# Hats from one product: offsets in three parts, positions and distance on 62 rows of a column of taps

## The chip, the core and the metric

The kernel runs on one core of a Trainium2 chip. The metric is the device time of one launch in microseconds (us), the median of three runs. One more execution was taken with the hardware profiler; its span is 7707.8 us, and all views of the profile are of that execution.

## The reference

Two layers work on x of 2 x 256 x 128 x 128 in fp32. What the change touches is in the first: a group norm, then three branches of deformable depthwise convolution with the dilations 1, 9 and 12. Each branch computes 18 offset planes by a 3x3 convolution (a y and an x offset for each of 9 taps), samples the normalised image bilinearly at the shifted positions, weighs the taps and sums them.

```python
def _branch(x, w_off, w_def, lw, lb, pad, dil):
    off = _conv(x, w_off, pad, dil)
    y = _deform_dw(x, off, w_def, pad, dil)   # bilinear samples at py, px, weighted per tap
    return jax.nn.gelu(_ln2d(y, lw, lb), approximate=False)
py = yy - pad + ky * dil + off[:, :, 0]
px = xx - pad + kx * dil + off[:, :, 1]
```

The branches and a 1x1 convolution are added, normalised, sent through an MLP and added to x. The second layer is a group norm and a 3x3 convolution with ternary weights.

## The kernel before

The kernel has three stages, one after the other. In the first (phase_a, for image 0 and then image 1) every group of four rows is normalised (tile xa), transposed by TensorE (tpa) and stored in a table of pixels (function columns); the same xa is multiplied with the weights of the offset convolutions (pz, copied to the ring zr). Every eight rows offsets adds up rows of zr (zs), shifts them by products with shift (po), and has 54 offsets for each pixel of eight rows (offs: 128 pixels of a row on the partitions, 8 rows, 54 planes).

A bilinear weight is a hat, 1 - min(1, |d|), of the distance d between a sampling position and a grid place. make_hats computes the weights of four rows (512 pixels) at all candidate places of all taps. The distance is linear: offset, plus where the pixel lies in a pattern of period 2 in y or 10 in x, plus a constant that depends on the place. So it is a product of a 0/1 matrix (hatw) with a matrix that has these numbers on its rows (planes). So that bf16 loses nothing, an offset is split in three bf16 parts which are added up by the product. The split is made on VectorE (DVE) at L395 to L398: round, subtract, round the rest, subtract. Parts are laid out with pixels on the partitions, so TensorE transposes them (pp, L407 and L408), and DVE copies the result to planes (L410, L411). pp, planes and hatw have two layers: in layer 0 the first parts of the 54 offsets and, from row 64, the second parts; in layer 1 the third parts and, from row 64, eight pattern rows. A layer of hatw has 648 columns: 27 taps with 24 places each.

For each of 3 columns of taps and 2 subsets of the 9 rows of taps (4 or 5) there is one bank of ph, made by two products that add up:

```python
for i, m in ((0, P), (1, HALF + NPAT)):
    nc.tensor.matmul(
        ph[0:n],
        lhsT=k["hatw"][0:m, i, h0 : h0 + n],
        rhs=pl[0:m, i, :],
        start=i == 0,
        stop=i == 1,
    )
```

The first takes 128 rows, the second 72. ScalarE (ACT) takes the absolute value (hb, L427), DVE does min and subtract (L428), and SyncE (SP) stores the bank to the array hats (L429). ph has two banks, pp one, hb eight buffers.

The order of the first stage is set by the framework's scheduler, which places each engine's instructions in a queue when the program is built; each engine runs its queue in order and waits by semaphores. At the end of the stage a flag is computed from the largest offset of both images, and the program branches on it. The second stage (sample_near) loads hats and table and does the sampling and what follows; its order on PE, ACT and DVE is written out by hand. The third is the second layer's convolution.

Of the kernel before, what the change touches and what calls it, by code (L numbers as in the profile page):

```python
# [19 lines left out]
P = 128  # L20
# [47 lines left out]
def conv_preact_kernel(ctx: ExitStack, tc: tile.TileContext, t: dict, out: bass.AP):  # L68
# [208 lines left out]
    def phase_a(b, pool, psum, k, beside):  # L277
# [53 lines left out]
        def offsets(G):  # L331


            po = psum.tile([P, 512], F32, name="po", tag="po", bufs=1)
            pov = po[:, 0 : ZG * NOFF].rearrange("p (r n) -> p r n", n=NOFF)
            zs = pool.tile([P, 3, ZG, 3 * 18], F32, name="zs", tag="zs", bufs=2)
            for br, dil in enumerate(DILS):

                def rows(ky, y, y1):

                    y, y1 = max(y, -ky * dil), min(y1, H - ky * dil)
                    while y < y1:
                        s = (y + ky * dil) % ZRING
                        n = min(y1 - y, ZRING - s)
                        z0 = (br * 3 + ky + 1) * 54
                        yield y, n, zr[:, s : s + n, z0 : z0 + 54]
                        y += n

                y0, y1 = G * ZG, (G + 1) * ZG
                for y, n, mid in rows(0, y0, y1):  # L350
                    done = y
                    for ya, na, up in rows(-1, y, y + n):
                        if ya > done:
                            nc.vector.tensor_copy(
                                zs[:, br, done - y0 : ya - y0], mid[:, done - y : ya - y]
                            )
                        nc.vector.tensor_tensor(
                            zs[:, br, ya - y0 : ya - y0 + na], mid[:, ya - y : ya - y + na], up,
                            ALU.add,
                        )  # L360
                        done = ya + na
                    if done < y + n:
                        nc.vector.tensor_copy(
                            zs[:, br, done - y0 : y + n - y0], mid[:, done - y : n]
                        )
                for y, n, down in rows(1, y0, y1):
                    dst = zs[:, br, y - y0 : y - y0 + n]
                    nc.vector.tensor_tensor(dst, dst, down, ALU.add)
            for br, dil in enumerate(DILS):
                for kx in range(3):  # L370
                    nc.tensor.matmul(
                        pov[:, :, br * 18 : br * 18 + 18],
                        lhsT=k["shift"][:, k["dxs"].index((kx - 1) * dil), :],
                        rhs=zs[:, br, :, kx * 18 : kx * 18 + 18],
                        start=br == 0 and kx == 0,
                        stop=br == 2 and kx == 2,
                    )
            offs = pool.tile([P, ZG, NOFF], F32, name="offs", tag="offs", bufs=2)
            nc.vector.tensor_copy(offs.rearrange("p r n -> p (r n)"), po[:, 0 : ZG * NOFF])
            i = b * (H // ZG) + G  # L380
            nc.vector.tensor_reduce(
                amax[:, i : i + 1],
                offs.rearrange("p r n -> p (r n)"),
                AX.X,
                ALU.max,
                apply_absolute_value=True,
            )
            nc.sync.dma_start(
                offd[b][G * ZG : (G + 1) * ZG].rearrange("r w n -> w r n"), offs
            )  # L390

            parts = k["parts"][G % 2]
            rest = pool.tile([P, ZG, NOFF], F32, name="rest", tag="rest", bufs=2)
            first, second = parts[:, 0, :, 0:NOFF], parts[:, 0, :, HALF : HALF + NOFF]
            nc.vector.tensor_copy(first, offs)  # L395
            nc.vector.tensor_tensor(rest, offs, first, ALU.subtract)
            nc.vector.tensor_copy(second, rest)
            nc.vector.tensor_tensor(parts[:, 1, :, 0:NOFF], rest, second, ALU.subtract)  # L398
            return parts

        def make_hats(g, parts, r0):


            pp = psum.tile([P, 2, NG], BF16, name="pp", tag="pp", bufs=1)
            for r in range(R):
                cols = slice(r * W, (r + 1) * W)
                nc.tensor.transpose(pp[:, 0, cols], parts[:, 0, r0 + r, :], ident_b)  # L407
                nc.tensor.transpose(pp[0:HALF, 1, cols], parts[:, 1, r0 + r, 0:HALF], ident_b)  # L408
            pl = k["planes"][g % 2]
            nc.vector.tensor_copy(pl[:, 0, :], pp[:, 0, :])  # L410
            nc.vector.tensor_copy(pl[0:HALF, 1, :], pp[0:HALF, 1, :])  # L411
            for tap in range(3):
                q0 = 0
                for nq in (4, 5):
                    n = nq * NH
                    h0 = (tap * 9 + q0) * NH
                    ph = psum.tile([P, 512], F32, name="ph", tag="ph", bufs=2)
                    for i, m in ((0, P), (1, HALF + NPAT)):
                        nc.tensor.matmul(  # L419
                            ph[0:n],  # L420
                            lhsT=k["hatw"][0:m, i, h0 : h0 + n],
                            rhs=pl[0:m, i, :],
                            start=i == 0,
                            stop=i == 1,
                        )
                    hb = pool.tile([P, NG], F32, name="hb", tag="hb", bufs=8)
                    nc.scalar.activation(hb[0:n], ph[0:n], AF.Abs)  # L427
                    nc.vector.tensor_scalar(hb[0:n], hb[0:n], 1.0, 1.0, ALU.min, ALU.subtract)  # L428
                    nc.sync.dma_start(  # L429
                        hats[b][q0 : q0 + nq, :, g * R : (g + 1) * R, tap].rearrange(  # L430
                            "q h r w -> (q h) r w"
                        ),
                        hb[0:n].rearrange("h (r w) -> h r w", w=W),
                    )
                    q0 += nq
# [11 lines left out]
    with ExitStack() as actx:  # L447
        psum = actx.enter_context(tc.tile_pool(name="ps_a", bufs=1, space=PSUM))

        def gps():  # L450
# [6 lines left out]
            "zero": ap.tile([P, C], F32, name="zero"),  # L457
            "wz": ap.tile([P, KC, NZ], F32, name="wz"),
            "shift": ap.tile([P, len(dxs), P], F32, name="shift"),
            "hatw": ap.tile([P, 2, NTAP * NH], BF16, name="hatw"),  # L460
            "parts": [ap.tile([P, 2, ZG, P], BF16, name=f"parts{i}") for i in range(2)],
            "zr": ap.tile([P, ZRING, NZ], F32, name="zr"),
            "planes": [ap.tile([P, 2, NG], BF16, name=f"planes{i}") for i in range(2)],
        }
# [5 lines left out]
        for b in range(NB):  # L470
            stats = ap.tile([P, KC, NGRP, 6], F32, name=f"stats1_{b}", tag=f"stats1_{b}")
            for c in range(KC):
                for g0 in range(0, NGRP, XT):
                    xt = ap.tile([P, XT * NG], F32, name="xt", tag="xt", bufs=3)
                    nc.sync.dma_start(
                        xt,
                        x[b, c * P : (c + 1) * P].rearrange("p h w -> p (h w)")[
                            :, g0 * NG : (g0 + XT) * NG
                        ],
                    )  # L480
                    for j in range(XT):
                        nc.vector.bn_stats(stats[:, c, g0 + j, :], xt[:, j * NG : (j + 1) * NG])
            if b == 0:
                load_now()
                nc.sync.dma_start(k["wz"], t["wz"].rearrange("(k p) n -> p k n", p=P))
                nc.sync.dma_start(k["shift"], t["shift"])
                hatw = ap.tile([P, 2, NTAP * NH], F32, name="hatw32", tag="xt", bufs=3)
                nc.sync.dma_start(hatw, t["hatw"])
                nc.vector.tensor_copy(k["hatw"], hatw)
                pattern = ap.tile([P, NG], F32, name="pattern", tag="xt", bufs=3)  # L490
                nc.sync.dma_start(pattern[HALF : HALF + NPAT], t["pattern"])
                for pl in k["planes"]:
                    nc.vector.tensor_copy(
                        pl[HALF : HALF + NPAT, 1, :], pattern[HALF : HALF + NPAT]
                    )
            mean, rstd = group_norm(stats, f"gn1_{b}", gps)
            gn1.append((mean, rstd))

            nc.vector.tensor_scalar(negmean[b], mean, -1.0, None, ALU.mult)
            for c in range(KC):  # L500
                nc.vector.tensor_scalar(
                    convs[b][:, c, :], convs[b][:, c, :], rstd[:, c : c + 1], None, ALU.mult
                )
            phase_a(b, ap, psum, k, beside)
# [810 lines left out]
```

## Time and profile before

| what | value |
|---|---|
| median of three runs | 7720.23 us (7712.4 to 7721.3) |
| span of the profiled execution | 7707.8 us |
| ph products L419 | 768, first at 115.3 us, last at 943.5 us |
| hats on ACT, L427 | 384, median 593 ns |
| transposes L407 and L408 | 256 each |
| casts L395 and L397, subtractions L396 and L398 | 32 each, medians 375, 377, 602 and 598 ns |
| PE, DVE, ACT busy over the whole span | 92%, 80%, 63% |

A line of a timeline gives the start in us, the duration in us, the engine, the line of the kernel, the operation, the tiles and how many instructions were merged. PE is TensorE's multiplication and PEld its loading of weights. The form 128*96 says that 128 rows and 96 columns of the array are active. A product's duration on PE contains its latency, so products in a row overlap in the record. In windows, "busy (x)" is the time in us in which an engine was busy and the number of its instructions. A product of fp32 stands as two records. The shares of busy time over the whole span mix three stages, so windows of the first stage are what counts here.

### The profile page before, as it was taken

Reading aid. Unit: us, or ns where it says so; the run is one execution under the profiler, and the core shown is the slowest. Engines: PE = TensorE matmul, PEld = TensorE weight load, DVE = VectorE, ACT = ScalarE, POOL = GpSimd, SP = SyncE. Lnnn points to the kernel's source line nnn. Section 1 sums busy time; section 2 is a strip of 40 time slices with the busy share of each in tenths; the row PEclk is TensorE's granted clock in tenths of the full one; section 3 lists DMA queues with packets and bytes.
Section 4 is the critical chain, followed back from the end, with each engine's and each line's share of the span. In section 5 each row is a group of like instructions: output and inputs, shape, how many; then the busy total and the mean of one; then the engine's idle time right before and its main releaser. Section 6 shows DMA issues by size and latency. Waiting matters only on the chain. (4 is left out here: it accounts for less than half of the span.)

```text
span 7707.8 us, 115349 instructions
## 1 busy us (share of the span) xinstructions
PE 7056.2 (92%) x37984; PEld 5364.4 (70%) x37984; DVE 6136.7 (80%) x12907; ACT 4821.4 (63%) x10150; POOL 716.3 (9%) x1292
## 2 busy tenths in 40 slices
PE   6899888999999999999988999999999999899999
PEld 3455477877877787877777877877788877444444
DVE  7666658888888888888578888888888886677676
ACT  2344356777777777777666777777777777433232
POOL 0000000111111111111100111111111111000000
PEclk9899989999999999999999999999999999899999
DMA  9867699999999999998689999999999996222121
GB/s 296 242 188 200 181 233 252 243 254 257 248 250 254 255 246 249 248 255 228 190 232 249 250 250 258 248 251 252 251 249 251 246 250 172 86 77 73 71 74 49
DMA packets 1012350, 1658.94 MB, mean 215 GB/s; under 512 B 120672, under 2 KB 573072, under 8 KB 1007512
## 3 DMA queue, kind: packets, MB, share of 16 engines
q1 hardware_dynamic: 994328, 1617.86, 78.2%
q10 hardware_dynamic: 17408, 33.56, 1.3%
q8 instruction: 304, 4.98, 0.3%
q14 instruction: 310, 2.54, 0.1%
HBM read 1381.02 MB, written 270.06 MB: 214 GB/s over the span
## 5 line engine op out<-in xcount | busy, mean ns | idle before, releaser
L886 PE MATMUL pm<-A,xs 128*128 128x180 f32 (+2 forms) x22288 | 3603.7, 317 | 467.9 <-ACT ev L895 435.2
L886 PEld LDWEIGHTS pm<-A,xs 128*128 128x128 f32 x22288 | 3399.3, 195 | 684.4 <-ACT ev L895 543.7
L864 DVE SCALAR_TENSOR_TENSOR ring<-ev,defw,ring 128x256 f32<-128x256 f32 (+3 forms) x6272 | 2775.7, 462 | 358.6 <-ACT ev L895 173.4
L895 ACT COPY ev<-pm 128x360 f32<-128x360 f32 (+2 forms) x5572 | 2238.5, 455 | 1125.7 <-DVE ring L864 453.7
L813 DVE TENSOR_TENSOR A<-hy,hx 128x768 f32<-128x768 f32 x1130 | 1021.3, 946 | 417.4 <-DMA hx<-hats 238.6
L1169 PE MATMUL pc<-cring,signs 128*128 128x512 bf16 x4608 | 1007.5, 382 | 20.0 <-ACT cring L1116 13.3
L1169 PEld LDWEIGHTS <-signs 128*128 128x128 bf16 x4608 | 452.4, 98 | 574.5 <-issue 30.1
L611 ACT ACTIVATE T<-T,rs 128x256 f32<-128x256 f32 x1280 | 662.4, 593 | 3.3 <-POOL rs L607 3.2
L604 POOL TENSOR_SCALAR rs<-mv 128x4 f32<-128x4 f32 x320 | 122.5, 383 | 4962.3 <-DVE mv L602 2297.5
L570 PE MATMUL hp<-T,w 128*128 128x512 f32 x1024 | 493.1, 606 | 13.8 <-ACT T L689 13.8
L600 DVE BATCH_NORM_STATS2 st<-T 128x6 f32<-128x256 f32 x1280 | 447.0, 412 | 24.0 <-ACT T L592 23.9
L320 PE MATMUL pz<-wz,xa 128*128 128x486 f32 x1024 | 462.8, 585 | 1.3 <-DVE zr L327 1.3
L570 PE MATMUL h<-hT,w 128*128 128x512 f32 x1024 | 460.1, 592 | 0.0
L639 ACT ACTIVATE T<-zc,bb,bw 128x512 f32<-128x512 f32 x384 | 279.2, 782 | 219.8 <-PE zc L623 215.4
L857 ACT ACTIVATE ring<-ev,defw 128x256 f32<-128x256 f32 (+1 forms) x788 | 392.2, 503 | 24.1
L623 PEld LDWEIGHTS zc<-ident,T 128*128 128x128 f32 x2560 | 323.4, 150 | 97.2 <-issue 61.4
L1177 ACT ACTIVATE o<-xl,l1b 128x1024 f32<-128x1024 f32 x64 | 73.5, 1148 | 502.0 <-DMA out_x<-o 384.6
L623 PE MATMUL zc<-ident,T 128*128 128x128 f32 x2560 | 365.9, 287 | 20.2 <-ACT T L611 14.1
L606 POOL TENSOR_TENSOR rs<-rs,mhalf 128x4 f32<-128x4 f32 x320 | 371.3, 1160 | 0.0
L1116 ACT CAST cring<-D 128x2048 bf16<-128x2048 f32 (+1 forms) x140 | 245.0, 1755 | 185.0 <-PE pc L1169 127.6
L592 ACT COPY T<-tp 128x512 f32<-128x512 f32 x640 | 341.9, 590 | 29.5 <-PE tp L590 29.2
L427 ACT ACTIVATE hb<-ph 96x512 f32<-96x512 f32 (+1 forms) x384 | 211.2, 592 | 183.0 <-PE ph L419 177.0
(118 smaller groups left out, 5258.8 us busy)
## 6 DMA issues: line engine op xcount, KB each, us to landing
hy<-hats SPq DMA_DIRECT2D x1114, 384.0 KB
hx<-hats SPq DMA_DIRECT2D x1114, 384.0 KB
xs<-table SPq DMA_DIRECT2D x1876, 128.0 KB
g12d<-T SPq DMA_DIRECT2D x128, 512.0 KB
other<-g12d SPq DMA_DIRECT2D x128, 512.0 KB
hats<-hb SPq DMA_DIRECT2D x192, 240.0 KB
hats<-hb SPq DMA_DIRECT2D x192, 192.0 KB
xl<-x1d SPq DMA_DIRECT2D x56, 640.0 KB
```

The costliest lines, as they stand in the source:

```text
L320: nc.tensor.matmul(pz[:, 0:NZ], lhsT=xt[:, c, r, :], rhs=k["wz"][:, c, :], start=c == 0, stop=c == KC - 1,)
L570: nc.tensor.matmul(out, lhsT=w, rhs=v, start=i == 0, stop=i == n - 1)
L600: pin(nc.vector.bn_stats(st[:, j, :], Tv[:, j, :]))
L606: nc.gpsimd.tensor_tensor(rs[:, 0, :], rs[:, 0, :], mhalf[:, 0:NB4], ALU.pow)
L611: nc.scalar.activation(Tv[:, j, :], Tv[:, j, :], AF.Identity, scale=rs[:, 0, j : j + 1], bias=rs[:, 1, j : j + 1],)
L623: nc.tensor.transpose(zc[:, j * P : (j + 1) * P], Tv[:, j, c * P : (c + 1) * P], ident)
L813: nc.vector.tensor_tensor(dst, hy[:, i0:i1].rearrange("p i t w -> p t i w"), hx[:, i0:i1].rearrange("p i t w -> p t i w"), ALU.mult,)
L857: pin(nc.scalar.mul(dst, src, w))
L864: pin(nc.vector.scalar_tensor_tensor(dst, src, w, dst, ALU.mult, ALU.add))
L886: nc.tensor.matmul(pm[:, j, 0:n], lhsT=xts[b, Rt][T + j][:, c * P : (c + 1) * P], rhs=A[:, m0:m1, AO + (T + j) * CI : AO + (T + j + 1) * C ...
L895: nc.scalar.copy(ev[:, m0:m1, T * CI : (T + 2) * CI].rearrange("p m (t j) -> p t m j", j=CI), pm[:, :, 0:n].rearrange("p t (m j) -> p t m ...
L1169: nc.tensor.matmul(pc[:, bank, :], lhsT=w[:, m * P : (m + 1) * P], rhs=xc[:, i, k, t * JC : (t + 1) * JC, kx : kx + W], start=j == 0, stop ...
```

## The change

The 54 offsets are ordered by column of taps: (n x) -> x n with x = 3. A column of taps has 18 offset planes. A block of 64 rows now holds all that this column's hats are made of: 18 first parts, 18 second parts, 18 third parts and 8 pattern rows, 62 rows in all. Blocks 0 and 1 lie on rows 0 to 63 and 64 to 127 of layer 0 of planes, block 2 on rows 0 to 63 of layer 1. A bank of ph is made by one product with 64 rows, at row 0 for columns 0 and 2 and at row 64 for column 1. The pattern no longer lies in planes but in parts, with pixels on the partitions, and is transposed with the offsets. hatw has one layer.

```diff
-            first, second = parts[:, 0, :, 0:NOFF], parts[:, 0, :, HALF : HALF + NOFF]
-            nc.vector.tensor_copy(first, offs)
-            nc.vector.tensor_tensor(rest, offs, first, ALU.subtract)
-            nc.vector.tensor_copy(second, rest)
-            nc.vector.tensor_tensor(parts[:, 1, :, 0:NOFF], rest, second, ALU.subtract)
+            blocks = parts.rearrange("p r (x n) -> p r x n", n=HALF)
+
+            def taken(i):
+                return blocks[:, :, :, i * (NOFF // 3) : (i + 1) * (NOFF // 3)]
+
+            def by_column(v):
+                return v.rearrange("p r (n x) -> p r x n", x=3)
+
+            nc.vector.tensor_copy(taken(0), by_column(offs))
+            nc.vector.tensor_tensor(by_column(rest), by_column(offs), taken(0), ALU.subtract)
+            nc.vector.tensor_copy(taken(1), by_column(rest))
+            nc.vector.tensor_tensor(taken(2), by_column(rest), taken(1), ALU.subtract)
...
-                nc.tensor.transpose(pp[:, 0, cols], parts[:, 0, r0 + r, :], ident_b)
-                nc.tensor.transpose(pp[0:HALF, 1, cols], parts[:, 1, r0 + r, 0:HALF], ident_b)
+                nc.tensor.transpose(pp[:, 0, cols], parts[:, r0 + r, 0 : 2 * HALF], ident_b)
+                nc.tensor.transpose(
+                    pp[0:HALF, 1, cols], parts[:, r0 + r, 2 * HALF : 3 * HALF], ident_b
+                )
...
-                    for i, m in ((0, P), (1, HALF + NPAT)):
-                        nc.tensor.matmul(
-                            ph[0:n],
-                            lhsT=k["hatw"][0:m, i, h0 : h0 + n],
-                            rhs=pl[0:m, i, :],
-                            start=i == 0,
-                            stop=i == 1,
-                        )
+                    rows = slice(tap % 2 * HALF, (tap % 2 + 1) * HALF)
+                    nc.tensor.matmul(
+                        ph[0:n],
+                        lhsT=k["hatw"][rows, h0 : h0 + n],
+                        rhs=pl[rows, tap // 2, :],
+                        start=True,
+                        stop=True,
+                    )
...
-            "hatw": ap.tile([P, 2, NTAP * NH], BF16, name="hatw"),
-            "parts": [ap.tile([P, 2, ZG, P], BF16, name=f"parts{i}") for i in range(2)],
+            "hatw": ap.tile([P, NTAP * NH], BF16, name="hatw"),
+            "parts": [ap.tile([P, ZG, 3 * HALF], BF16, name=f"parts{i}") for i in range(2)],
...
-                pattern = ap.tile([P, NG], F32, name="pattern", tag="xt", bufs=3)
-                nc.sync.dma_start(pattern[HALF : HALF + NPAT], t["pattern"])
-                for pl in k["planes"]:
-                    nc.vector.tensor_copy(
-                        pl[HALF : HALF + NPAT, 1, :], pattern[HALF : HALF + NPAT]
-                    )
+                pattern = ap.tile([P, ZG, NPAT], F32, name="pattern", tag="xt", bufs=3)
+                nc.sync.dma_start(pattern, t["pattern"])
+                for parts in k["parts"]:
+                    for i in range(3):
+                        at = i * HALF + NOFF
+                        nc.vector.tensor_copy(parts[:, :, at : at + NPAT], pattern)
```

The rest of the diff fills pattern and hatw on the host in the new order.

More of the change, by code (lines that the diff above doesn't have):

```diff
@@ L486, in conv_preact_kernel @@
                 nc.sync.dma_start(k["shift"], t["shift"])
-                hatw = ap.tile([P, 2, NTAP * NH], F32, name="hatw32", tag="xt", bufs=3)
+                hatw = ap.tile([P, NTAP * NH], F32, name="hatw32", tag="xt", bufs=3)
                 nc.sync.dma_start(hatw, t["hatw"])
                 nc.vector.tensor_copy(k["hatw"], hatw)
-                pattern = ap.tile([P, NG], F32, name="pattern", tag="xt", bufs=3)
-                nc.sync.dma_start(pattern[HALF : HALF + NPAT], t["pattern"])
-                for pl in k["planes"]:
-                    nc.vector.tensor_copy(
-                        pl[HALF : HALF + NPAT, 1, :], pattern[HALF : HALF + NPAT]
-                    )
+                pattern = ap.tile([P, ZG, NPAT], F32, name="pattern", tag="xt", bufs=3)
[4 more added lines that the diff above has]
+                        nc.vector.tensor_copy(parts[:, :, at : at + NPAT], pattern)
             mean, rstd = group_norm(stats, f"gn1_{b}", gps)
@@ L1250 @@
     shift = np.stack([px[:, None] == px[None, :] + dx for dx in dxs], 1).astype(np.float32)
-    pattern = np.ones((NPAT, R, W), np.float32)
+    pattern = np.ones((W, ZG, NPAT), np.float32)
     for m in range(RI):
-        pattern[m] = ((np.arange(R) + REACH + m) % RI)[:, None]
+        pattern[:, :, m] = ((np.arange(ZG) + REACH + m) % RI)[None, :]
     for i, m in enumerate(XCLS):
-        pattern[RI + i] = ((np.arange(W) + REACH + m) % CI)[None, :]
-    hatw = np.zeros((P, 2, NTAP * NH), np.float32)
+        pattern[:, :, RI + i] = ((np.arange(W) + REACH + m) % CI)[:, None]
+    hatw = np.zeros((P, NTAP * NH), np.float32)
     ybase = np.zeros((H, NTAP), np.float32)
@@ L1263 @@
             for comp, size, m in ((0, TR, dy % RI), (1, TC, RI + XCLS.index(dx % CI))):
-                plane = br * 18 + comp * 9 + tap
+                base = tap % 3 % 2 * HALF
+                plane = (br * 18 + comp * 9 + tap) // 3
                 for r in range(size):
                     h = (n % 3 * 9 + n // 3) * NH + comp * TR + r
-                    hatw[[plane, HALF + plane], 0, h] = 1.0
-                    hatw[[plane, HALF + m], 1, h] = 1.0
-                    hatw[HALF + NPAT - 1, 1, h] = REACH - r
+                    for part in range(3):
+                        hatw[base + part * (NOFF // 3) + plane, h] = 1.0
+                    hatw[base + NOFF + m, h] = 1.0
+                    hatw[base + NOFF + NPAT - 1, h] = REACH - r
             ybase[:, n] = np.arange(H) + dy
@@ L1277 @@
         "shift": shift,
-        "pattern": pattern.reshape(-1, NG),
+        "pattern": pattern,
         "hatw": hatw,
```

## The prediction

> **What bounds the kernel now.** I first looked for the stage that holds the change. The tile view of ph gives its instructions between 115 and 944 us of the 7707.8 us span, and none later; this is the first stage, in which both images are normalised, transposed and turned into hats. Then I asked for the busy time in windows of that stage.
>
> ```profile
> core 0: us, PE busy (x) PEld busy (x) DVE busy (x) ACT busy (x) POOL busy (x), PEclk, DMA share, GB/s
> ...
> 600.00:700.00 100.00, 99.66 (x416) 56.50 (x416) 66.00 (x149) 42.37 (x79) 0.00 (x0) 1.00 0.72 196
> 700.00:800.00 100.00, 99.69 (x419) 56.46 (x418) 64.29 (x144) 42.52 (x80) 0.00 (x0) 1.00 0.71 196
> ...
> 900.00:950.00 50.00, 39.69 (x189) 22.31 (x188) 31.81 (x77) 22.19 (x40) 0.78 (x1) 0.95 0.72 183
> 240.00:400.00 160.00, 138.72 (x531) 74.63 (x530) 111.72 (x237) 53.70 (x102) 0.00 (x0) 0.91 0.81 238
> ```
>
> In the second image PE is busy 99.7 of 100 us at full clock, with DVE at 65, ACT at 42 and DMA at 0.72. A round of eight rows (two calls of columns, one of offsets, two of make_hats) takes 25.6 us from one L395 to the next, and 20 of the 32 rounds have about that period. Elsewhere PE is not the limit: between 240 and 400 us it is busy 139 of 160, DVE waits there for xa's loads, and rounds take 33 us; after 920 us ACT and the stores of hats set the pace. The next stage reads a flag made from all offsets and the hats of both images, so what the PE-bound rounds lose or win moves the end one for one. Later stages have the same instructions on PE, DVE, ACT and SP in both programs, in the same order.
>
> Then the price of a hat product, from the tile view of ph:
>
> ```profile
> L419 PE MATMUL ph<-planes,hatw x768: 376/379/634, 115.3 to 943.5; 128*96 128x512 bf16 x192
> L427 ACT ACTIVATE hb<-ph x384: 583/593/622, 116.2 to 944.0; 96x512 f32<-96x512 f32 x192
> ```
>
> A product is recorded with 379 ns, but that holds its latency. What it costs PE is the step from start to start: four in a row last 1.03 us, so (1.03 - 0.38) / 3 = 0.217 us. Four products also keep their loads (PEld) out of the way.
>
> Last, what it costs PE to change the shape of the tile that it computes on. The change makes ph run on 64 rows; no product here does that yet. But L408 does on columns: it writes 64 of 128. The PE timeline of one piece shows it:
>
> ```profile
> 494.95 0.64 PE L419 MATMUL ph<-planes,hatw 128*96 128x512 bf16 x2
> 495.42 0.22 PE L407 MATMUL pp<-ident_b,parts 128*128 128x128 bf16 x1
> 495.48 0.59 PE L419 MATMUL ph<-planes,hatw 128*120 128x512 bf16 x2
> 496.00 0.24 PE L408 MATMUL pp<-ident_b,parts 128*64 128x128 bf16 x1
> 496.18 0.23 PE L407 MATMUL pp<-ident_b,parts 128*128 128x128 bf16 x1
> ...
> 492.33 0.24 PE L408 MATMUL pp<-ident_b,parts 128*64 128x128 bf16 x1
> 492.50 1.08 PE L320 MATMUL pz<-wz,xa 128*128 128x486 f32 x2
> ```
>
> L407, 128 columns wide like its neighbours, hands over after 0.06 us (495.42 to 495.48). The second ph of 495.48 starts at 495.48 + 0.59 - 0.38 = 495.69, and L408 follows at 496.00: 0.31 us instead of 0.217, so 0.09 us to enter the other shape. L408 itself takes 0.17 us (492.33 to 492.50) where a stream of 128 columns took 0.06: 0.11 us, of which I put some 0.02 to its own load and 0.09 to leaving. And the first pass of pz after it lasts 1.08 - 0.57 = 0.51 us, against 0.98 - 0.57 = 0.41 in undisturbed pairs: 0.10 us, because its load could not run ahead. A ph after L408 loses 0.04 us that way.
>
> [...] loads of hatw start some 0.4 us ahead behind a pz. [...] the casts with a step of 3 should stay at 0.375 us.
>
> **The change part by part.**
>
> Removed: one of two products per bank of ph, 384 x 0.217 = -83.3 us of PE. ACT still makes 384 hats at 0.593 us and the stores are the same.
>
> Added: visits to a 64-row tile. In the order of the changed program the 384 products stand in 239 groups (115 single, 120 of two, a few longer) between whole-array instructions. A visit costs 0.09 to enter, 0.04 for its own load, 0.09 to leave, and the exposed load of what follows. 179 visits end at pz, tpa or po (fp32, 0.10): 0.32 us each, 58 us. 35 end at a transpose of L407's kind, behind which the next load starts after 0.06 us and which I give 0.02: 0.24 each, 8 us. 25 end, but for one, at a transpose of L408's kind, which had to be entered from another shape anyway: 0.14, 4 us. Together +70 us, from neighbours on the other axis: the bounds are 0 (rows need no drain) and 153 us (below).
>
> Gained beside it: at 51 places a product on rows 64 to 127 meets one on rows 0 to 63 in the same shape. If they run side by side each hides one: -11 us, or 0 if not. I take -11.
>
> PE's balance is -83 + 70 - 11 = -24 us. Only the PE-bound rounds give it to the end; with 20 of 32 fully and a few in part I take 0.7: -17 us.
>
> Moved: transposes. Each first transpose now needs the third part too, so DVE's chain from po to pp grows by the last subtraction (L398 before), 0.60 us: 0.61 + 0.60 + 0.38 + 0.60 + 0.38 + 0.60 = 3.2 us, and 0.66 for a zr copy between. The changed order puts 8 tpa and 5 pz (4.9 us) there instead of 8 and 3 (3.3 us), so the 0.2 us that L407 waits in a full round (at 622.20 us pz hands over to it after 0.60 us instead of 0.41) should go: -4 us in 20 rounds. Queued behind a late transpose are pz and ph, and ACT behind those; so in the last two rounds of each image, where nothing stands between, it costs 4 x 0.6 = +2 us.
>
> On DVE, the casts could [...] take the 0.60 us of the subtraction: up to 2 x 0.22 us per round, in an engine that is 65% busy and with 0.8 us of room: 0 to +3 us, I take 0. The six copies of pattern and the cast of half as many weights lie between 67 and 100 us, hidden by pz: 0 (bounds -1 to +1). hatw's load is 324 KB smaller; nothing waits for it (cast at 67.2, first use at 115), but DMA is 0.9 busy there: 0 to -2 us, I take -1. The smaller memset of parts is hidden by the first loads. No queue is passed by another on SP but the stores of hats and table, which change places with each other.
>
> Sum: -17 - 4 + 2 - 1 = -20 us. On this execution's span 7707.8 becomes 7688; the three timed runs (7712.4 to 7721.3) have a median 12.4 us above that span, so 7720 becomes 7700.
>
> **The rivals.** *Rows are free.* A 64-row tile could need no drain. For it: only columns are shown to drain. [...] Then PE would lose 94 us; in bursts of hats ACT then binds (two hats and half a zr copy, 1.19 + 0.28 us, against 0.43 + 0.81 of PE), so about 0.6 of it reaches the end: -55 us, 7665.
>
> *Rows drain dearer, and the kernel is slower.* The place is each of the 239 visits: if the array empties fully, entering and leaving cost the whole latency beyond the stream[...] and both loads (0.12 and 0.19) lie bare: 0.64 us, 153 us in all, against 83 saved with no overlap: +70, of which 0.7 reaches the end, 7769. The balance turns at 94 / 239 = 0.39 us a visit, or 0.35 without overlap; I have 0.29 on average. With 0.45 it would be 7738. For it: the margin is thin. Against it: L408 shows less.
>
> *The saving is hidden.* If xa's loads and DVE set more of the rounds than I think, or ACT's banks of ph (two) become the wait, nothing moves: 7715 to 7722. Against it are the windows with PE at 99.7.
>
> **How the numbers follow.** Drain as with columns: 0.55, spread 7685 to 7715. Rows free: 0.20. Dearer drain: 0.18. Hidden: 0.07. A measurement of this kernel tells 0.2% (15 us) from no change. Faster by more: 0.31 of the first case, all of the second, 0.01 of the last: 0.52. Within: 0.23 + 0.05 = 0.28. Slower: 0.01 + 0.18 + 0.01 = 0.20. The likeliest case's own range is 7685 to 7715; for 8 in 10 the range takes in most of the free case and the nearer half of the dear one, 7650 to 7745.
>
> **What would show it.** Right: in the PE timeline, pz to ph in 0.50 us, ph's last to pz in about 0.31 to 0.35, pz's first pass 0.51; a full round of 25.0 us or a little less instead of 25.6; rows 64 followed by rows 0 within some 10 ns. The drain is wrong if loads of hatw still start ahead behind pz, or if those steps exceed 0.6 us. The whole argument is wrong if the time after 950 us changes, or if PE is no longer over 95% busy in the second image while the rounds still last 25.6 us.

## The result, and the profile after

The changed kernel takes 7757.0 us (median of four runs, 7753.8 to 7758.4), beside 7720.8 for the kernel before (7712.4 to 7721.4). The ratio is 1.0049, interval 1.0031 to 1.0066: slower by half a per cent. The forecast was faster, 7700 us, and the measured time lies above its range, which ended at 7745. The profiled execution of the changed kernel has a span of 7755.9 us, 48.2 more than before's.

All of that arises in the first stage. The last hat on ACT ends at 993.6 us where it ended at 944.6, 49 us later; from there to the end it takes 6762.2 us, and took 6763.2. The first 13 rounds of each image took 379 and 333 us before and take 388 and 360; the stretch from the first image's last split to the second image's first grew from 57 to 68. Over all rounds, some 25 of the 49 us lie in the second image, 8 in the first, 11 in that stretch and 4 after the last split.

The windows of the first stage, as for the kernel before (columns: window and length; PE, PEld, DVE, ACT, POOL busy; PE clock; DMA share; GB/s):

```profile
600.00:700.00 100.00, 95.22 (x348) 46.44 (x348) 63.92 (x141) 40.24 (x76) 0.00 (x0) 0.95 0.72 197
700.00:800.00 100.00, 96.99 (x349) 45.80 (x350) 63.41 (x140) 41.31 (x77) 0.00 (x0) 0.95 0.67 182
800.00:900.00 100.00, 92.52 (x323) 44.27 (x321) 56.87 (x123) 34.05 (x63) 0.00 (x0) 0.88 0.62 168
```

PE is no longer busy throughout (99.7 before), and its clock, which was 1.00, is 0.88 to 0.95. At half clock two passes of pz take 1.99 us where they otherwise take 1.08 (both below), and PE counts as busy throughout, so the first number hides part of the loss. DVE and ACT are busy for less of each window than before, and DMA for no more: no other engine has become full over a window. Something interrupts PE. Its waits between 560 and 900 us name what (line waited for: us in total, times, longest):

```profile
DVE xa L173 <- DMA xa<-in_x: 17.7, 16, 2.9
PE pz L320 <- DVE zr L327: 15.0, 11, 3.1
```

PE waits 11 times until DVE has copied a bank of pz to zr. Before, that wait did not occur there at all, and DVE's wait for xa's loads was 13.1 us in 12 times. Two timelines show the chain. First the kernel before; "SPq" and "ACTq" lines are DMA issues, a "x12" is twelve of them from the start given:

```profile
602.81 11.06 SPq L429 DMA_DIRECT2D hats<-hb  x12
...
608.69 0.39 ACTq L296 DMA_DIRECT2D xa<-in_x  x1
...
613.51 0.55 DVE L173 TENSOR_SCALAR xa<-xa,gn_mean,gn_rstd 128x512 f32<-128x512 f32 x1 [0.56 <-DMA xa<-in_x]
...
617.18 0.37 ACTq L296 DMA_DIRECT2D xa<-in_x  x1
...
620.65 0.38 DVE L395 CAST parts<-offs 128x432 bf16<-128x432 f32 x1
620.94 0.54 DVE L173 TENSOR_SCALAR xa<-xa,gn_mean,gn_rstd 128x512 f32<-128x512 f32 x1
```

A round loads xa twice. DVE waits for the first of the two, here 0.56 us at 613.51; all 12 waits of the kernel before between 560 and 900 us are for a first load, and PE does not feel them. The second load goes out at 617.18, 8.5 us after the first and some 4 us after the last store of hats. DVE needs it inside the split, at 620.94, and finds it there. Between 617.2 and 621 the DMA share is 0.53. Now the changed kernel:

```profile
812.32 10.23 SPq L438 DMA_DIRECT2D hats<-hb  x11
...
819.42 0.37 ACTq L296 DMA_DIRECT2D xa<-in_x  x1
...
824.36 1.38 SPq L438 DMA_DIRECT2D hats<-hb  x1
...
825.79 0.38 ACTq L296 DMA_DIRECT2D xa<-in_x  x1
...
829.26 0.44 DVE L402 CAST parts<-offs 128x432 bf16<-128x432 f32 x1
...
832.10 0.55 DVE L173 TENSOR_SCALAR xa<-xa,gn_mean,gn_rstd 128x512 f32<-128x512 f32 x1 [2.40 <-DMA xa<-in_x]
...
834.01 0.67 DVE L327 COPY zr<-pz 128x486 f32<-128x486 f32 x1
834.73 1.29 PE L320 MATMUL pz<-wz,xa 128*128 128x486 f32 x2 [2.53 <-DVE zr L327]
...
837.70 1.99 PE L320 MATMUL pz<-wz,xa 128*128 128x486 f32 x2
```

The second load goes out 6.4 us after the first and 1.4 us after the last hats store was issued; the DMA share until 832.1 is 0.87. DVE waits 2.40 us for it at its place in the split, the zr copy queued behind comes late, and PE, which needs that bank, stands 2.53 us. In each of the nine rounds from 604 to 832 us DVE waits so for the second load. From soon after PE's wait to 856 us PE runs at half clock: the two passes of pz at 837.70 take 1.99 us, where undisturbed ones take 1.08.

### The profile page after: what moved, and what is told of

The parts are those of the page before. It is cut to its first block, busy times and chain, and to the rows that moved or that the text cites. A ratio compares the mean times of both kernels' runs of the same rounds, so it can differ in the third digit from the quotient of the medians.

```text
span 7755.9 us, 114589 instructions
## 1 busy us (share of the span) xinstructions
PE 7084.5 (91%) x37600; PEld 5313.8 (69%) x37600; DVE 6148.2 (79%) x12911; ACT 4818.5 (62%) x10150; POOL 713.4 (9%) x1292
## 5 line engine op out<-in xcount | busy, mean ns | idle before, releaser
L320 PE MATMUL pz<-wz,xa 128*128 128x486 f32 x1024 | 513.1, 629 | 46.2 <-DVE zr L327 46.1
```

The lines of the kernel that those rows point to most:

```text
L320: nc.tensor.matmul(pz[:, 0:NZ], lhsT=xt[:, c, r, :], rhs=k["wz"][:, c, :], start=c == 0, stop=c == KC - 1,)
```

## The experiments

Three explanations were open: that visits to a 64-row tile are dearer than priced; that DVE holds PE up (its slower split, or the order with five pz between po and the transposes); that xa's loads come late. Ratios are to the kernel before in the same series of runs. Single runs of one kernel spread widely (the kernel before from 7693 to 7745 us in a series of 63), so only the intervals tell how firm a difference is.

**One product on all 128 rows.** hatw holds zeros in the rows of the other column, rows 64 to 127 of layer 1 of planes are cleared once, and a bank is still one product, with no visit to another shape.

```diff
-                        lhsT=k["hatw"][rows, h0 : h0 + n],
-                        rhs=pl[rows, tap // 2, :],
+                        lhsT=k["hatw"][:, h0 : h0 + n],
+                        rhs=pl[:, tap // 2, :],
...
+        for pl in k["planes"]:
+            nc.vector.memset(pl[HALF:, 1, :], 0.0)
```

> The changed kernel, with the one product of each bank of ph on all 128 rows (the other column's rows of hatw are zero, rows 64 to 127 of the second layer of planes are zeroed once). The same numbers are computed and the order on PE is that of the changed kernel, but no product changes the shape of the tile. Theory A (the visits to 64 rows ate what the removed products saved; the rest of the loss is DVE's wait for xa, which lets PE stall on zr and its clock halve): the steps pz to ph 0.41 instead of 0.50 us, ph to pz 0.22 instead of 0.35; PE has 60 us less to do (71 of visits less, 11 of side-by-side products given back), but the waits for zr and the spells at half clock stay, so 7757 becomes about 7715, with at least three spells of half clock left in the second image. Theory B (64 rows by themselves make the clock drop): no spell of half clock in the second image, about 7680. Theory C (DVE's slower strided split is the loss): waits as before the edit, about 7715 too, told apart by the third run.

Measured: 7689.5 us, 0.9963 (0.9953 to 0.9972), some 67 us below the changed kernel. That is near what the prediction gave the visits (70 less 11), but the waits differ in the two kernels, so it is no clean price; the rounds below give one. But this kernel has 2.6 us less PE work in each round than before by the same working, 83 us in all, and gains only 29. Its waits between 560 and 900 us:

```profile
DVE xa L173 <- DMA xa<-in_x: 35.7, 16, 4.1
PE pz L320 <- DVE zr L327: 32.5, 11, 4.2
```

Both waits are twice as long as in the changed kernel, with no 64-row tile anywhere. The less PE has to do, the longer they are. The clock is 0.90 to 0.93 in the windows from 560 to 860 us, so 64-row tiles are not what lowers it; the time itself lies between what I expected with the spells of half clock (7715) and without them (7680).

**A fifth buffer for xa**, in the changed kernel and, as a control, in the kernel before.

```diff
-            xt = pool.tile([P, KC, R, W], F32, name="xa", tag="xa", bufs=4)
+            xt = pool.tile([P, KC, R, W], F32, name="xa", tag="xa", bufs=5)
```

> The changed kernel with five buffers for xa instead of four, so that each load is asked for one group of rows earlier; PE's order is the same. Theory A: DVE's waits for xa and PE's waits for zr over 1 us vanish in the second image, the clock stays at 1.0 there, rounds of 25.0 us or less; 7757 becomes 7705 to 7730. Theory B: the waits vanish but the clock still drops, 7745 to 7757. Theory C: 7745 to 7757 with waits of PE for zr left.

> Control: the kernel before with five buffers for xa. Its second image has hardly a wait to lose (25.6 us a round), so only the rounds of 33 us in the first image shorten: up to 5 x 7 us, 7690 to 7715. If it gains as much as the changed kernel does by the same edit, the late loads are no property of the change.

Measured: 7749.3 us, 1.0043 (1.0032 to 1.0054), and for the control 7717.5 us, 1.0001 (0.9991 to 1.0012). In the changed kernel PE still waits 12.7 us for zr copies, and a load is still normalised 5 to 6 us after its issue: the scheduler moved the normalisation with the load. The experiment did not take the wait away, and decides nothing on it. The changed kernel's time fell where I had put the other theories, the control's 2 us above what I expected.

**The split read contiguously.** The planes stand in the wrong order by this, so the hats are computed from other taps' offsets; work and shapes are the same.

```diff
-                return v.rearrange("p r (n x) -> p r x n", x=3)
+                return v.rearrange("p r (x n) -> p r x n", x=3)
```

> The changed kernel with the split reading offs and rest in their own order (18 neighbours at a time instead of every third). The planes then come in the wrong order, so the hats are of other taps' offsets; the work is the same. Theory C: the casts return to 0.375 and the subtractions to 0.60 us, 0.42 us less per round in front of zr and pp; PE's waits for zr and the spells of half clock vanish and the time falls by 20 us or more. Theories A and B: the durations fall, the time by at most 13 us (32 rounds of 0.42), 7744 to 7757.

Measured: 7736.7 us, 1.0032 (1.0021 to 1.0043). Casts and subtractions are back at 377, 379, 602 and 601 ns. That is 13 us less than the changed kernel by the ratios, though their intervals overlap; PE still waits 11.8 us in 10 times for zr copies. The step of 3 costs something, and is not the main cause.

**Loads in a tile of their own.** Three buffers take the loads and two the normalised groups, so a load is issued about a round ahead, and the scheduler puts both normalisations ahead of the split. The same in the kernel before.

```diff
-            xt = pool.tile([P, KC, R, W], F32, name="xa", tag="xa", bufs=4)
+            xl = pool.tile([P, KC, R, W], F32, name="xl", tag="xl", bufs=3)
+            xt = pool.tile([P, KC, R, W], F32, name="xa", tag="xa", bufs=2)
...
-                normalise(xt[:, c], xt[:, c], mean[:, c : c + 1], rstd[:, c : c + 1])
+                normalise(xt[:, c], xl[:, c], mean[:, c : c + 1], rstd[:, c : c + 1])
```

> The changed kernel with xa in two tiles: loads go to xl (three buffers), the normalised rows to xa (two buffers). DVE's order then has no normalisation between the split's four steps, and a load has some 12 us before it is needed. The edit before it (a fifth buffer) had left the load and the wait where they were, 5 to 6 us apart. Theory A (late loads hold DVE, DVE holds PE on zr, and after a stall of over some 1.4 us PE runs at half clock for 10 to 20 us): PE's waits for zr over 1 us and the spells of half clock are gone from the rounds of the second image, which take 24.4 to 25.0 us; 7700 +- 10, 40 to 60 us less than the changed kernel. Theory B (64 rows make the clock drop): spells stay, 7735 or more. Theory C (the split's own slower steps): stalls and spells stay in half the rounds, 7730.

> Control: the kernel before with the same two tiles. Its second image stays at 25.6 us a round; in the first image the five rounds of 33 us shorten where the late loads caused them, by 0 to 30 us: 7690 to 7716. The prediction's balance of PE work (24 us for the change) is tested by the difference of the run beside it and this one: 10 to 24 us in favour of the change if the sum was right and only the waits were missed; against the change by 10 us or more if the visits cost more than was counted.

Measured: the changed kernel with it 7678.1 us, 0.9955 (0.9938 to 0.9973); the kernel before with it 7673.0 us, 0.9962 (0.9948 to 0.9976). Late loads had cost the kernel before 0.38% (29 us, most of it in the first image, whose rounds fell from 33 to 25 to 29 us) and the changed kernel 0.94% (73 us). The difference, 44 us, is more than the 38 us by which the change lost; the intervals leave some 20 us of doubt on it. Both kernels are faster than I expected, and the 10 to 24 us in favour of the change that I expected between them did not show: it is 5 us by the ratios, and 5 us against the change by the medians. In the changed kernel's second image the clock is back at 1.00, no wait for zr is left, and PE's largest wait is that for the split, about once a round:

```profile
PE pp L415 <- DVE parts L406: 4.7, 14, 1.3
```

This edit takes the normalisations out of the split too. Their place alone is not the cause: in the kernel before they stand in the split as well (620.94 above), and PE does not wait.

**All zr copies on ACT**, in the changed kernel with its loads as they were, so that the wait cannot go by way of DVE's zr copies.

```diff
-                (nc.scalar.copy if r % 2 else nc.vector.tensor_copy)(
+                nc.scalar.copy(
```

> The changed kernel with all copies of pz to zr on ACT (half of them were on DVE). DVE still waits for the loads of xa in the middle of the split, but it no longer frees pz's banks. If PE is held only by way of zr, its waits of over 1 us and the spells of half clock go: 7690 to 7715. If DVE's wait reaches PE by the split as well (pp waits for the last subtraction), waits of 1 to 2 us for parts appear in their place and spells of half clock stay: 7725 to 7755.

Measured: 7739.4 us, 1.0026 (1.0016 to 1.0037). No wait for a zr copy on DVE is left, and the wait comes by another way:

```profile
DVE xa L173 <- DMA xa<-in_x: 53.8, 15, 5.5
...
PE po L371 <- DVE zs L368: 12.0, 11, 1.7
```

DVE waits longer for xa than in any other kernel, and PE waits for the sums zs queued behind. It is the first load of a round that is late here: one goes out at 598.08, 0.06 us after a hats store, and is normalised at 604.18, after a wait of 4.38 us. The second load follows the last hats store by some 4 us and is on time in all rounds but one. Moving the copies gave back 18 us of the loss by the ratios (the intervals overlap), and the profiled execution has a clock of 1.00 from 560 to 860 us. Late loads reach PE by more than one way.

**The order alone.** In the kernel before, the transpose of the third parts goes first, so that the first transpose waits for the last subtraction. PE's order then has 8 tpa and 5 pz between po and the transposes, exactly as in the changed kernel, with products, shapes and split of before. The second kernel is the same with the loads in their own tile.

```diff
-                nc.tensor.transpose(pp[:, 0, cols], parts[:, 0, r0 + r, :], ident_b)
                 nc.tensor.transpose(pp[0:HALF, 1, cols], parts[:, 1, r0 + r, 0:HALF], ident_b)
+                nc.tensor.transpose(pp[:, 0, cols], parts[:, 0, r0 + r, :], ident_b)
```

> The kernel before, with nothing changed but that of each pair of transposes the one of the third parts goes first, so that the first transpose waits for the last subtraction. Its PE order then has 8 tpa and 5 pz between po and the first transpose, as in the changed kernel, where before has 3 pz. Products, tiles' shapes and split are those of before. If the order alone brings the waits (my theory: the fourth and fifth pz need banks that DVE, held up by a late xa in the split, has not yet freed), PE's waits for the zr copies come up in the second image with 8 to 15 us in 560 to 900 us (none before), some rounds take 28 to 33 us instead of 25.6, and the kernel is slower than before by 15 to 45 us. If the waits come from the 64-row products or the slower split, PE's waits stay below 2 us there, the rounds at 25.6 us, and the time within 0.2% of before.

> The same exchange of the two transposes, in the kernel with xa's loads in a tile of their own (three buffers for the loads, two for the normalised groups). If the order hurts only through late loads, the time is that of the kernel before with the same loads, 0.994 to 0.998 of before, and the rounds of the second image take 25.4 to 25.7 us. If the order costs by itself (the transposes wait longer for the third parts), each round is 0.4 us or more longer and the time 0.998 or above.

Measured: 7705.9 us, 0.9996 (0.9986 to 1.0006), and with the loads apart 7683.0 us, 0.9965 (0.9954 to 0.9977). My theory at that point, that the order with five pz brings the waits by itself, falls. A window of the first of the two:

```profile
560.00:660.00 100.00, 99.84 (x416) 55.82 (x415) 64.58 (x142) 39.41 (x74) 0.00 (x0) 1.00 0.66 178
```

PE is full, at full clock, and waits 0.2 us for a zr copy in all of 560 to 900 us. (No run has late loads with the old order, so the order may still be needed for the wait to reach PE.) What this kernel keeps from before is the time of the loads: its second load also goes out 8.5 us after the first and 4.0 to 5.0 us after the last hats store. Over the kernels, the second image shows:

| kernel | second load after first | after last hats store (most rounds) | DVE waits for xa, 560 to 900 us | PE waits for zr there |
|---|---|---|---|---|
| before | 8.5 us | 4.2 to 4.9 us | 13.1 us | none |
| before, third parts first | 8.5 | 4.0 to 5.0 | 13.7 | 0.2 |
| changed, contiguous split | 6.4 | 1.1 to 2.2 | 15.0 | 11.8 |
| changed | 6.4 | 1.2 to 2.1 | 17.7 | 15.0 |
| one product on 128 rows | 5.9 | 0.1 to 0.8 | 35.7 | 32.5 |

This is the theory that remains. The DMA share (the number before the last) from a round's first load on, before and, below the dots, after:

```profile
608.70:613.50 4.80, 4.75 (x20) 2.74 (x19) 3.36 (x8) 2.77 (x6) 0.00 (x0) 1.00 1.01 283
613.50:617.20 3.70, 3.70 (x11) 1.73 (x10) 2.70 (x5) 0.59 (x2) 0.00 (x0) 1.00 1.05 316
617.20:621.00 3.80, 3.80 (x29) 3.34 (x28) 2.09 (x5) 1.57 (x3) 0.00 (x0) 1.00 0.53 165
...
819.40:825.40 6.00, 6.00 (x15) 2.63 (x16) 3.50 (x8) 2.26 (x5) 0.00 (x0) 1.00 1.00 287
825.80:832.10 6.30, 6.30 (x34) 4.28 (x32) 2.80 (x7) 1.62 (x3) 0.00 (x0) 1.00 0.87 250
```

The stores of a round, six of hats with 192 KB, six with 240 KB and those of 512 KB to the table, are the same in both kernels, and the DMA engines are full in both for a time from the first load on: for 8.5 us before (1.01 and 1.05, at 283 and 316 GB/s), for 6.0 us after (1.00, at 287 GB/s). Before, no hats store is issued in the 4 us ahead of the second load. The DMA engines are not idle then (1.05); they work off what is queued, and the load, at 617.2, finds them half free (0.53, its own transfer included). With less work on PE it goes out while they are still full (1.00 up to 825.4, 0.87 from 825.8 on). It is then normalised 4.4 to 6.3 us after its issue (the nine rounds from 604 to 832 us), where it was 3.7 to 4.0 us before, and the wait runs from DVE to PE.

**The best of the parts.** The single product on 128 rows with the loads apart; then also with planes in column order from the start, so that the split reads contiguously (weights wz reordered on the host, po written in that order, the largest-offset test reading it so); then that second form with the 64-row products of the change.

```diff
-                return v.rearrange("p r (n x) -> p r x n", x=3)
+                return v.rearrange("p r (x n) -> p r x n", x=3)
...
-        "wz": offw.transpose(3, 0, 4, 2, 1).reshape(C, NZ),
+        "wz": offw.reshape(3, 3, 3, 2, C, 9).transpose(4, 0, 5, 2, 3, 1).reshape(C, NZ),
```

> One product on all 128 rows (zeros for the other column) and xa in two tiles. Theory A: 60 us of PE work less than the run with 64 rows and two tiles, and no stalls: 7640 to 7660. If removing the stalls lets another wait appear (ACT's copies of ph, loads), 7660 to 7690.

> The same with the offset planes put in the order of the columns of taps by the weights and by where po is written, so that the split reads neighbours: casts 0.375 and subtractions 0.60 us again. Theory A: 0 to 5 us less than the run without (DVE no longer holds PE up). Theory C: 15 us or more less.

> The changed kernel (64 rows) with xa in two tiles and the offset planes in the order of the columns of taps, so that the split reads neighbours. Neither late loads nor slower split steps are left, only the removed products and the visits to 64 rows. The prediction's PE balance (24 us of gain over 32 rounds, 0.75 a round) is then seen bare against the kernel before with two tiles (7673, 25.4 us a round in the second image): 24.6 to 24.7 us a round and 7650 to 7668. If rounds stay at 25.0 or more, the visits cost more than the balance says.

Measured: 7629.4 us, 0.9895 (0.9878 to 0.9912); 7612.5 us, 0.9871 (0.9851 to 0.9890); and with 64-row products 7678.3 us, 0.9949 (0.9931 to 0.9966). The first two are faster than I expected. The second is the fastest of all, 1.3% below the kernel before, and 17 us below the first by the medians, where I had expected 0 to 5. The last has nothing but the change in it, with loads and split out of the way:

```profile
560.00:660.00 100.00, 99.94 (x381) 49.42 (x380) 66.60 (x150) 43.19 (x81) 0.00 (x0) 1.00 0.76 205
```

PE is full, and the rounds of the second image take 24.6 us, beside 25.4 for the kernel before with the same loads and 25.3 with the third parts first as well: 0.6 to 0.7 us per round in the mean of 13, where the prediction's balance is 24 / 32 = 0.75. Over the whole kernel little of it is left, 0.9949 beside 0.9962 and 0.9965, all three intervals overlapping, and 7678 us where I had expected 7650 to 7668. The first image still has three rounds of 31 to 33 us, and the stretch between the images takes 64 us instead of the 59 of the kernel before with the same loads; the clock is at half for 20 us of it, there for 7.

## Why the prediction was wrong

**The visits: right.** PE's timeline of an undisturbed piece of the changed kernel:

```profile
602.30 1.08 PE L320 MATMUL pz<-wz,xa 128*128 128x486 f32 x2
603.32 0.42 PE L428 MATMUL ph<-planes,hatw 64*120 64x512 bf16 x2
603.67 1.90 PE L320 MATMUL pz<-wz,xa 128*128 128x486 f32 x4
605.50 0.42 PE L428 MATMUL ph<-planes,hatw 64*120 64x512 bf16 x1
605.85 4.35 PE L320 MATMUL pz<-wz,xa 128*128 128x486 f32 x10
```

The second pz starts at 602.30 + 1.08 - 0.57 = 602.81, and ph follows at 603.32: 0.51 us, predicted 0.50. From ph back to pz it is 0.35 us both times, predicted 0.31 to 0.35, and the first pass after it takes 0.51. The load of hatw starts with ph, both at 603.32, where before it started 0.41 us ahead behind a pz (493.01, for ph at 493.42). The two products at 603.32, one on each half of the rows, end within 0.42 us, which is the time of one; two on the same half take 0.64. In the trace the second of such a pair starts 3 to 4 ns after the first. So here a change of shape took about as long for rows as for columns (0.10 us to enter 64 rows, 0.09 for 64 columns), and products on the two halves ran side by side. The traces show how long a change takes, not what the array does in that time; "drain" in the prediction is a name for it. The rival of a dearer drain had 7738 to 7769, where the time fell, but by luck: a visit that ends at pz cost (0.51 - 0.41) + (0.35 - 0.217) + (0.51 - 0.41) = 0.33 us, predicted 0.32, where that rival had 0.64. (Its 0.64 is an estimate; with the prediction's reading of 0.217 us for a product's stream it is 2 x (0.379 - 0.217) + 0.12 + 0.19 = 0.63.) Nor are rows free: ph followed pz after 0.51 us, not 0.41.

**Removed and added: right in sum, both parts smaller.** From the kernel before with third parts first (25.3 us a round) to one product on 128 rows with a contiguous split (23.1), loads apart in both, a round lost 2.2 us; predicted 83 / 32 = 2.6. The 64-row form (24.6) gives back 1.5; predicted (70 - 11) / 32 = 1.8.

**Moved: right for the full rounds, too small for the ends of the images.** The step was "the 0.2 us that L407 waits in a full round should go: -4 us". The order alone has rounds of 25.4 us where before has 25.6. The +2 us of the last rounds is not in their length, 18.3 and 3.8 us where it was 18.6 and 4.6, but behind them. After the first image's last split PE waits for the last subtraction, and its clock is at half for the next 30 us (in the second line, a window, the number after the last count is the clock):

```profile
PE pp L414 <- DVE parts L405: 1.4, 1, 1.4
...
521.50:552.10 30.60, 28.87 (x68) 10.61 (x68) 18.69 (x50) 14.25 (x26) 1.02 (x1) 0.50 0.66 168
```

Before, that wait is 0.4 us and the clock there is 1.00. The stretch between the images is 11 us longer, and the end after the second image's last split 4 us: 15 us, where the prediction had 2. All nine kernels with one product per bank have this wait, 1.2 to 1.4 us, then 17 to 31 us at half clock, and take 61 to 68 us for the stretch; the five others have no wait of 1 us there, 0 to 7 us at half clock, and take 57 to 59. No run takes the wait away alone, so that it brings the clock down is not shown.

**The split: wrong.** The step was "the casts with a step of 3 should stay at 0.375 us", with up to 3 us in all. All four instructions are longer, and I had not priced the subtractions at all (min/median/max in ns):

```profile
L402 DVE CAST parts<-offs x32: 431/450/466, 110.1 to 970.5; 128x432 bf16<-128x432 f32 x32
L403 DVE TENSOR_TENSOR rest<-offs,parts x32: 727/742/756, 111.1 to 972.3; 128x432 f32<-128x432 f32 x32
```

With 446 and 728 ns for the other two the split grew by 0.41 us a round (375, 602, 377 and 598 before). That the casts would keep their time was an estimate, which no run had shown for this step. With the loads apart the contiguous split takes 0.4 us off each round of the second image, 25.0 to 24.6 with 64 rows and 23.5 to 23.1 with 128. That is some 12 us over 32 rounds, near the 13 us by the ratios of the contiguous split above, where I took 0 and at most 3.

**What sets the rounds: the step that failed.** It was "Only the PE-bound rounds give it to the end; with 20 of 32 fully and a few in part I take 0.7: -17 us". It took the share of PE-bound rounds from before as fixed, and PE's work as independent of the loads. (The share was read too high as well: 16 rounds of before lie within 0.5 us of 25.6, and two more at 27.) I had seen the loads bind in the first image, and the rival "the saving is hidden" named them, but with 7715 to 7722, no loss. In fact the second load of each round of the second image was on time only because PE was slow: the DMA engines had 4 us between the last hats store and the load to work off their queue. The changed kernel leaves them 1 to 2 us, and the loads' cost rises from 29 to 73 us by the ratios. The prediction's own sign for this came: PE is 92 to 97% busy, and these rounds take 27.7 us in the mean. What is left of the change with the loads apart, 5 us less by the ratios and 5 more by the medians, cannot be told from nothing. In those two profiles the second image's rounds are 6 us shorter in all; the first image's are 6 us longer, and the stretch and the end 8 us.

**What makes the wait dear: the clock.** The prediction has no term for it. In the 13 rounds of the second image late loads cost 359.6 - 325.3 = 34 us (changed kernel, loads as they are and apart). The waits are 15 us of it; the other 19 I put to products at half clock after a wait, as the timeline at 837.70 shows them. Four spells, 55 us together, lie in these rounds; two of them:

```profile
671.70:681.80 10.10, 10.10 (x22) 3.24 (x21) 4.10 (x10) 2.75 (x5) 0.00 (x0) 0.50 0.25 63
835.50:855.90 20.40, 20.40 (x46) 7.35 (x45) 7.61 (x19) 7.62 (x14) 0.00 (x0) 0.50 0.40 99
```

Where the clock stayed at 1.00, the waits cost no more than themselves. The profiled execution of the contiguous split has waits of 11.8 us, none over 1.7, a clock of 1.00, and 332.3 us for these rounds; with the loads apart and a contiguous split they take 320.5, which is 11.8 less. That execution is the fastest of its kernel's 20 runs, with a mean clock of 0.967; the slowest takes 66 us more, at 0.961. So the clock differs from one execution to the next.

Not settled: whether it is the stores that delay the load, which the times argue, since no run moved or spread the stores alone; whether the wait for the last subtraction lowers the clock between the images; and what decides whether a wait of 1 to 2 us is followed by half clock.

## What to carry to other kernels

Before crediting work taken off a full engine, look at what was landing or leaving under it: mark each DMA issue in a round, how long after the last store of a burst it goes out, and how much earlier it will be issued and needed once the engine is faster. A load that arrives just without a wait can be a bound that no view of waits shows: before, DVE found the second load at 620.94 in place, and in the changed kernel it waits 2.40 us for it at 832.10. And if the load can be issued a round ahead, do that first: here that gave 0.4% by itself, and with it one product on all rows, with the planes in column order, gave a further 0.9%.

## What the runs showed of the hardware

- A tile of 64 rows took 0.10 us to enter (0.51 us from an fp32 product to ph, where the stream is 0.41), near the 0.09 of 64 columns; from ph to an fp32 product, whose load starts only with it (both at 603.67), it was 0.35 us from start to start. Zeros in the other 64 rows were cheaper than that: a round with full-height products took 23.1 us, with 64-row products 24.6.
- Short waits were followed by half clock on PE for longer than they lasted, though not all of them. In the changed kernel's second image waits of 1.41, 1.52, 2.53 and 3.06 us were followed within 2 us by 10, 10, 20 and 14 us at half clock, and one of 1.81 us by none. It is no effect of 64-row tiles alone: the kernel with one product on 128 rows has 51 us of it in its second image.
- A step of 3 elements in fp32 operands cost DVE 0.07 us in a cast of 432 elements per partition (450 and 446 ns, beside 375 and 377) and 0.13 to 0.14 us in a subtraction (742 and 728 ns, beside 602 and 598).
